# The second feed-forward stage by quarters of 256 positions instead of halves of 512, its gates and results among the steps of the delta loop

## The chip, the cores and the metric

The kernel runs on 1 core of one Trainium2 chip. The metric is the device time of the run in microseconds (us). Engines are named as in the profile: PE (matmul), DVE (vector), ACT (activations), POOL (elementwise and selects), SP (which issues most DMAs).

## The reference

Four blocks follow each other on `x` of shape (4, 1024, 256): attention, a feed-forward block, a gated delta-rule block, and the same feed-forward block again with the same weights.

```python
x = x + attn_a(layernorm(x), ...)
x = x + ffn(layernorm(x), ...)
x = x + attn_b(layernorm(x), ...)   # delta rule
x = x + ffn(layernorm(x), ...)

def ffn(x, wf, uf, bf, wi, ui, bi, wc, uc, bc, wo, uo, bo, in_c):
    c0 = broadcast(in_c)
    def step(c, xt):
        ft = sigmoid(xt @ wf.T + c @ uf.T + bf)
        it = sigmoid(xt @ wi.T + c @ ui.T + bi)
        gt = tanh(xt @ wc.T + c @ uc.T + bc)
        return ft * c + it * gt
    c_final = scan(step, c0, x)             # over the first axis
    return tanh(x @ wo.T + c_final @ uo.T + bo)
```

The recurrence of the feed-forward block runs over the first axis, the 4 batches, and is independent for each of the 1024 positions. The output of every position in every batch needs the cell after batch 3. The delta rule runs along the 1024 positions with one state per batch and head:

```python
kb = kc * bc[:, None]
A = tril(kb @ kc.T, -1)
U = solve_triangular(eye + A, vc * bc[:, None] - kb @ S, lower=True)
o = qc @ S + tril(qc @ kc.T) @ U
S = S + kc.T @ U
```

## The kernel before

Attention comes first and fills the first half of the run. The rest is `feed_and_delta`: the first feed-forward stage, the delta loop, the second feed-forward stage, with the last gates of the first stage and the first gates of the second laid among the steps of the loop. The order of all instructions on all engines is written out by hand (`tc.manual_schedule()`): each engine takes its instructions in the order in which the code issues them.

**The delta loop** (L1226) takes steps `s` from 0 to 50. A tile is 32 positions of all four batches, 32 tiles in all, and four tiles make a block of 128 positions. Step `s` makes the keys, queries, values and gates of tile `c = s` (to step 31), the score products of tile `s - 1`, and the recurrence of tile `t = s - 18` (`LAG` is 18): `from_state` (L808, 64 small matmuls with the state), `less` (L824, DVE), `solve` (L835, with the inverse loaded by `place`), `state` (L849, 32 small matmuls and a DVE sum `sb`), `within` (L862). One step behind, for tile `s - 19`, come `turn_out` (L889, two transposes of the scaled output `og`) and `result` (L907, the product with `wo`, then a POOL add; after every fourth tile `x3` is written to DRAM). The inverses of 8 tiles at a time are computed on DVE by `substitute`, cut over seven steps; the last group runs in steps 34 to 40. Steps 32 and on have no keys.

**The gates** of a feed-forward stage (`half_gates`, L929) are made for 512 positions at a time. For each batch `t` (0 to 3), each half `m` of the 256 cell features and each gate `j` (f, i, c) there is a part `begin` (L942), two matmuls 128x128 by 128x512 with the normalized input `k.xnT`, and for `t > 0` a part `end` (L956), two more with the cell of batch `t - 1` added into the same PSUM tile. The profile counts each of these matmuls twice, so a part appears as x4. `act` (L965) is the tanh on ACT, `combine` (L976) the new cell on DVE (and POOL for batch 0). Both are put off in `cells.late` and issued by `flush` at the beginning of the next part. A half has 42 parts and two that only flush. With two PSUM banks (`steps_banks`) two `begin`s stand ahead of their `end`s; with one bank they alternate.

PSUM tiles of the loop come from the pool `pps` of three buffers (tag `ps1`): the products of keys and gates, transposes, output products, norm transposes, gate tiles (in the loop) and results. `solve` has a buffer of its own (`pzu`).

**The results** of a stage: `extra` (L1030) is the product of the final cell with `uo` for 128 positions, into `e`; `residual` (L1042) loads 128 positions of all batches (512 KB); `fed` (L1047) is, for one batch, the product with `wo`, a DVE add of `e`, a tanh and a POOL add to the residual, and after batch 3 a write of 512 KB. `settle` issues the tanh and POOL adds that are owed. For positions 512 to 1023 of the second stage `ahead` (L1080) makes the products with `wo` before the cell is known, and `last_results` (L1098) adds the rest at the end.

**The second stage before the change.** The input of 128 positions `q` is loaded and normalized (`second_norm`, L1166) in two halves of two batches; `later` (L1219) gives their steps: q0 in steps 32 and 33, q1 in 34 and 35, q2 in 36 and 37, q3 in 38 and 39, q4 in 42 and 43, q5 in 46 and 47, the first half of q6 in 50. The load of q is issued three steps before its first half (L1298). `SECOND` is therefore 40: from there `half_gates(0)` gives three parts to each step through `gate_part` (L1242), in up to four slots: ahead of `solve`, behind it, behind `turn_out`, behind `result`. 33 parts are done by the end of step 50. After the loop `woven` lays the last 11 parts of the first half among the norms of q6 and q7, then `half_gates(1)` (44 parts, 42 with matmuls) among the results of q0 to q3 and the `ahead` work of q4 to q7, and `last_results` ends the run.

```python
                if s >= SECOND:
                    fill, gates = gates[:3], gates[3:]
```

Of the kernel before, what the change touches and what calls it, by code (L numbers as in the profile page):

```python
# [491 lines left out]
def feed_and_delta(k, w, out):  # L492
# [19 lines left out]
    W = TT + 1  # L512
    with ExitStack() as es:
        wp = es.enter_context(tc.tile_pool(name="d_w", bufs=1))
        hp = es.enter_context(tc.tile_pool(name="d_h", bufs=4))
        big = es.enter_context(tc.tile_pool(name="d_big", bufs=1))
        sm = es.enter_context(tc.tile_pool(name="d_sm", bufs=1))
        kp = es.enter_context(tc.tile_pool(name="d_keep", bufs=LAG))
# [407 lines left out]
        cells = Ctx()  # L926
        e = wp.tile([P, NTL // BT // 2, C], F32, name="e")

        def half_gates(n, banks, cellp):  # L929


            cells.bank, cells.late = 0, []
            of = [[] for _ in range(B)]
            cells.new = of[B - 1]

            def flush():
                now, cells.late = cells.late, []
                for a in now:
                    a()

            def begin(t, m, j):
                flush()  # L942
                if j == 0:
                    cells.act, cells.ps = [], {}
                pool, tag = banks[cells.bank % len(banks)]
                cells.bank += 1
                ps = cells.ps[j] = pool.tile([P, 512], F32, tag=tag, name="ps_gate")
                for kc in range(KC):
                    nc.tensor.matmul(  # L949
                        ps, f["w" + "fic"[j]][:, kc, ds(m * P, P)], k.xnT[:, kc, t, ds(n * 512, 512)],  # L950
                        start=kc == 0, stop=t == 0 and kc == KC - 1,
                    )
                if t == 0:
                    cells.late.append(lambda: act(t, m, j))

            def end(t, m, j):  # L956
                flush()
                for kc in range(KC):
                    nc.tensor.matmul(  # L959
                        cells.ps[j], f["u" + "fic"[j]][:, kc, ds(m * P, P)], cellp.get(of[t - 1], kc),  # L960
                        start=False, stop=kc == KC - 1,
                    )
                cells.late.append(lambda: act(t, m, j))

            def act(t, m, j):  # L965
                bias = f[("z" if t == 0 else "b") + "fic"[j]]
                a = gp.tile([P, 512], F32, tag="g", name="gate")
                nc.scalar.activation(  # L968
                    a, cells.ps[j], AF.Tanh, bias=bias[:, m : m + 1], scale=0.5 if j < 2 else 1.0
                )  # L970
                cells.act.append(a)
                if j == 2:
                    acts = cells.act
                    cells.late.append(lambda: combine(t, m, acts))

            def combine(t, m, acts):  # L976

                nc.vector.scalar_tensor_tensor(acts[1], acts[1], 1.0, acts[2], ALU.add, ALU.mult)  # L978
                new = cellp.new(of[t], m)
                if t == 0:  # L980
                    nc.vector.tensor_scalar(
                        acts[0], acts[0], 1.0, f["in_c"][:, m : m + 1], ALU.add, ALU.mult
                    )
                    nc.gpsimd.tensor_tensor(new, acts[0], acts[1], ALU.add)
                else:
                    nc.vector.scalar_tensor_tensor(
                        acts[0], acts[0], 1.0, cellp.get(of[t - 1], m), ALU.add, ALU.mult
                    )
                    nc.vector.scalar_tensor_tensor(new, acts[0], 0.5, acts[1], ALU.mult, ALU.add)

            parts = []
            for t in range(B):
                for m in range(KC):
                    first = [lambda t=t, m=m, j=j: begin(t, m, j) for j in range(3)]
                    second = [lambda t=t, m=m, j=j: end(t, m, j) for j in range(3)] if t > 0 else []
                    if len(banks) > 1 and t > 0:
                        parts += [first[0], first[1], second[0], second[1], first[2], second[2]]
                    elif t > 0:
                        parts += [a for j in range(3) for a in (first[j], second[j])]
                    else:  # L1000
                        parts += first
            parts.append(flush)
            parts.append(flush)
            return parts

        class OfRing:
# [6 lines left out]
            def get(self, cur, m):  # L1013
                return cur[m]

        class OfBlocks:


            def new(self, new, m):
                if m == 0:  # L1020
                    new.append(hp.tile([P, KC, BT, B, TT], F32, tag="h", name="cell"))
                return self.get(new, m)

            def get(self, cur, m):
                return cur[0][:, m].rearrange("p c b t -> p (c b t)")

        of_ring, of_blocks = OfRing(), OfBlocks()
        steps_banks = [(pzu, "zu"), (pps, "ps1")]

        def extra(q, cellp, new):  # L1030

            ps = pps.tile([P, C], F32, tag="ps1", name="ps_e")
            for kc in range(KC):
                nc.tensor.matmul(
                    ps, cellp.get(new, kc)[:, ds(q % 4 * P, P)], f["uo"][:, kc, :], start=kc == 0,
                    stop=kc == KC - 1,
                )
            nc.vector.tensor_tensor(e[:, q % 4, :], ps, f["bo"], ALU.add)

# [1 line left out]

        def residual(q, x, name):  # L1042

            posns[q].x = io.tile([P, B, C], F32, tag="xi", name=name)
            nc.sync.dma_start(out=posns[q].x, in_=x[:, ds(q * P, P), :].rearrange("b p d -> p b d"))

        def fed(q, b, to, bank=(pps, "ps1")):  # L1047
# [28 lines left out]
        def fed_at_once(q, b, to):  # L1076
            fed(q, b, to)()
            settle()

        def ahead(q, i):  # L1080

            p = posns[q]
# [15 lines left out]
        def last_results(new):  # L1098
# [6 lines left out]
                    out=out[ds(2 * i, 2), ds(q * P, P), :].rearrange("b p d -> p b d"), in_=x  # L1105
                )

            for q in range(NTL // BT // 2, NTL // BT):
                ps = pps.tile([P, C], F32, tag="ps1", name="ps_e")
                for kc in range(KC):  # L1110
                    nc.tensor.matmul(
                        ps, of_blocks.get(new, kc)[:, ds(q % 4 * P, P)], f["uo"][:, kc, :],
                        start=kc == 0, stop=kc == KC - 1,
                    )
                for i, (x, h) in enumerate(posns[q].ahead):
# [28 lines left out]
        def last_norms():  # L1144
# [1 line left out]
            o = Ctx()  # L1146

            def get(n):
                o.x = io.tile([P, 4, C], F32, tag="xi", name="xl")
                nc.sync.dma_start(  # L1150
                    out=o.x, in_=k.x1[B - 1, ds(n * 512, 512), :].rearrange("(n p) d -> p n d", p=P)
                )
# [20 lines left out]
        with tc.manual_schedule():  # L1173
            NQ = NTL // BT

            woven(half_gates(0, steps_banks, of_ring), last_norms())
            new = cells.new
            gates = half_gates(1, steps_banks, of_ring)
            LEAD = 12
            shadows = [lambda q=q: extra(q, of_ring, new) for q in range(NQ // 2)]  # L1180
            for q in range(2):
                shadows.append(lambda q=q: residual(q, k.x1, "x1"))
                shadows += [lambda q=q, b=b: fed_at_once(q, b, k.x2) for b in range(B)]
# [35 lines left out]
            later = {}  # L1219
            for q in range(NQ):  # L1220
                for i in range(2):
                    s = max(NTL + 2 * q + i, BT * q + LAG + 8 + i)
                    if s < NTL + LAG + 1:
                        later[s] = (q, i)
            SECOND = max(s for s, (q, i) in later.items() if q == 3) + 1
            for s in range(NTL + LAG + 1):  # L1226
                c = s if s < NTL else None
                c1 = s - 1 if 0 <= s - 1 < NTL else None
# [5 lines left out]
                normed = n < len(blocks) and i < 2  # L1234
                convolved = n < len(blocks) and i >= 2
                fill = places.get(s, [])
                if s == SECOND:
                    gates = half_gates(0, [(pps, "ps1")], of_blocks)
                if s >= SECOND:
                    fill, gates = gates[:3], gates[3:]  # L1240

                def gate_part():  # L1242
                    if fill:
# [32 lines left out]
                    keys(c)  # L1276
                else:
                    gate_part()
                substitute(s, 0.7)
                if t is not None:  # L1280
                    solve(t)
# [20 lines left out]
                    within(t)  # L1302
                    scale(t)
                if GATES <= s < GATES + 4:
                    extra(s - GATES + 4, of_ring, cells.new)
                adds = [fed(q, b, k.x2, bank) for q, b in feeding]
                if normed and i == 0:
                    stats(blocks[n], 1)
# [22 lines left out]
                if convolved:  # L1331
                    silu(n, i - 2)

            rest = [(q, i) for q in range(NQ) for i in range(2) if (q, i) not in later.values()]
            shadows = []
            for q, i in rest:
                if i == 0 and q not in [a for a, _ in later.values()]:
                    shadows.append(lambda q=q: residual(q, k.x3, "x3"))
                shadows += second_norm(q, i)
            woven(gates, shadows)  # L1340
            new = cells.new
            shadows = [lambda q=q: extra(q, of_blocks, new) for q in range(NQ // 2)]
            for q in range(NQ // 2):
                shadows.append(lambda q=q: residual(q, k.x3, "x3"))
                shadows += [lambda q=q, b=b: fed_at_once(q, b, out) for b in range(B)]
            for q in range(NQ // 2, NQ):
                shadows += [lambda q=q, i=i: ahead(q, i) for i in range(2)]
            woven(half_gates(1, steps_banks, of_blocks), shadows)
            last_results(cells.new)


# [99 lines left out]
```

## Time and profile before

| | us |
|---|---|
| median of 3 runs | 1451.28 (1450.35 to 1452.29) |
| the profiled execution | 1450.73 |
| its span, first to last instruction | 1448.9 |
| PE busy | 1360.6 |
| DVE / ACT / POOL busy | 803.8 / 681.8 / 420.8 |
| start of step 32, 40, 48 (its `from_state`) | 1140.64, 1208.62, 1287.17 |
| last gate matmul ends | 1430.16 |

All times of the profile are from one execution, and parts of it are compared with its own time. The start of a step is the first of the 64 `from_state` matmuls (L819). PE's granted clock is given as a share of full speed.

### The profile page before, as it was taken

To read this page: it belongs to the slowest core of one execution; us is meant where nothing else is said; L and a number is where in the kernel's file an instruction comes from. 1 tells how busy PE (TensorE), PEld (TensorE's weight loads), DVE (VectorE), ACT (ScalarE), POOL (GpSimd) and SP (SyncE) were. 2 spreads that over 40 slices of the span, in tenths; PEclk is the share of its full clock that TensorE was granted. 3 is DMA by queue.
4 is the path that set the end of the run, shared out by engine and by line. 5 is a ranking of instruction groups with operands and counts; after the bars stand their busy time and mean duration, and the time that the engine had idled before them with its cause. 6 is when DMAs were issued, how large, how long until landed. Compare 5 with 4: busy or idle time off the path is not lost. (4 is left out here: it accounts for less than half of the span.)

```text
span 1448.9 us, 33556 instructions
## 1 busy us (share of the span) xinstructions
PE 1360.6 (94%) x13316; PEld 660.6 (46%) x13316; DVE 803.8 (55%) x2298; ACT 681.8 (47%) x1639; POOL 420.8 (29%) x680
## 2 busy tenths in 40 slices
PE   7999999999999999999999989988788878999997
PEld 3443444434444343344344545454455555554554
DVE  5775667666676666676322333377777665233224
ACT  2365655556555656555632244455454333334222
POOL 4030002323032120021120233256676655342221
PEclk8899999999999999999999999999999769999999
DMA  3203111101110001100020121234545544221032
GB/s 95 53 16 79 17 18 43 20 2 46 32 32 17 2 17 31 32 17 2 17 74 15 44 66 52 67 95 107 132 117 121 127 117 97 55 66 44 29 92 97
DMA packets 117804, 79.78 MB, mean 55 GB/s; under 512 B 58960, under 2 KB 114768, under 8 KB 117648
## 3 DMA queue, kind: packets, MB, share of 16 engines
q1 hardware_dynamic: 115616, 76.33, 21.2%
q8 instruction: 105, 1.72, 0.5%
q10 hardware_dynamic: 2032, 1.31, 0.3%
q14 instruction: 51, 0.42, 0.1%
HBM read 41.37 MB, written 27.59 MB: 48 GB/s over the span
## 5 line engine op out<-in xcount | busy, mean ns | idle before, releaser
L337 ACT ACTIVATE p<-ps_s 128x512 f32<-128x512 f32 (+3 forms) x768 | 334.0, 491 | 249.0 <-PE ps_s L325 215.8
L325 PE MATMUL ps_s<-k,q 32*128 32x512 f32 (+3 forms) x1536 | 393.4, 541 | 2.7 <-DVE m L341 1.1
L330 PE MATMUL ps_s<-q,k 32*128 32x512 f32 (+3 forms) x1536 | 351.0, 532 | 0.0
L347 DVE TENSOR_REDUCE m<-ps_s 128x1 f32<-128x512 f32 x256 | 163.9, 685 | 83.3 <-PE ps_s L325 76.9
L341 DVE CUSTOM_DVE_ANT_0 junk<-ps_s,mask,m 128x512 bf16<-128x512 f32 (+3 forms) x256 | 128.1, 548 | 71.8 <-PE ps_s L325 70.9
L379 PE MATMUL ps_y<-p,vb 128*32 128x512 f32 (+3 forms) x1536 | 163.3, 498 | 1.2 <-ACT ys L385 1.2
L325 PEld LDWEIGHTS ps_s<-k,q 32*128 32x128 f32 x1536 | 149.4, 185 | 26.0 <-issue 9.4
L330 PEld LDWEIGHTS ps_s<-q,k 32*128 32x128 f32 x1536 | 121.7, 183 | 81.0 <-DVE m L347 20.1
L341 DVE CUSTOM_DVE_ANT_0 junk<-ps_s,mask 128x512 bf16<-128x512 f32 (+3 forms) x256 | 114.8, 487 | 72.9 <-PE ps_s L325 60.1
L403 POOL TENSOR_TENSOR xa<-xa,yt 128x256 f32<-128x256 f32 x32 | 23.3, 728 | 312.9 <-DVE yt L399 300.0
L322 PEld LDWEIGHTS <-identb 128*128 128x128 bf16 x512 | 34.6, 98 | 116.0 <-issue 112.4
L164 POOL TENSOR_SCALAR rs<-mv 128x2 f32<-128x2 f32 x24 | 5.5, 228 | 272.1 <-DVE mv L163 272.1
L379 PEld LDWEIGHTS ps_y<-p,vb 128*32 128x32 f32 x1536 | 30.6, 108 | 105.2 <-issue 92.0
L655 PE MATMUL ps_kqv<-wa,h 128*128 128x512 f32 x128 | 67.3, 642 | 8.2 <-ACT h L645 8.2
L322 PE MATMUL ps_s<-mb,identb 128*128 128x128 bf16 x512 | 71.4, 223 | 0.3 <-ACT p L337 0.3
L978 DVE SCALAR_TENSOR_TENSOR gate<-gate 128x512 f32<-128x512 f32 x32 | 22.8, 712 | 85.5 <-ACT gate L968 85.5
L1063 POOL TENSOR_TENSOR x<-x,hh 128x256 f32<-128x256 f32 x48 | 37.5, 787 | 98.4 <-ACT hh L1062 75.1
L1058 DVE TENSOR_TENSOR hh<-ps_h,e 128x256 f32<-128x256 f32 x48 | 20.2, 420 | 80.0 <-PE ps_h L1052 73.0
L949 PE MATMUL ps_gate<-xnT,ffn_wf 128*128 128x512 f32 x128 | 61.0, 599 | 1.0 <-DVE yt L399 1.0
L949 PE MATMUL ps_gate<-xnT,ffn_wc 128*128 128x512 f32 x128 | 60.8, 597 | 0.1
L949 PE MATMUL ps_gate<-xnT,ffn_wi 128*128 128x512 f32 x128 | 60.4, 594 | 0.0
L169 POOL TENSOR_SCALAR xn<-xa,mv,rs 128x256 f32<-128x256 f32 x48 | 58.4, 1225 | 2.5
(208 smaller groups left out, 2172.4 us busy)
## 6 DMA issues: line engine op xcount, KB each, us to landing
x<-x SPq DMA_DIRECT2D x28, 512.0 KB
kept<-gs SPq DMA_DIRECT2D x32, 192.0 KB
gl<-kept SPq DMA_DIRECT2D x32, 192.0 KB
x<-xa SPq DMA_DIRECT2D x8, 512.0 KB
xb<-x SPq DMA_DIRECT2D x32, 128.0 KB
xr<-x SPq DMA_DIRECT2D x32, 128.0 KB
x<-xr SPq DMA_DIRECT2D x32, 128.0 KB
k<-kall SPq DMA_DIRECT2D x60, 64.0 KB
```

Of the source, the lines that this page charges most:

```text
L169: nc.gpsimd.tensor_scalar(xn, bt.xa[:, c + i, :], mv[:, i, 0:1], rs[:, i : i + 1], ALU.subtract, ALU.mult)
L322: nc.tensor.matmul(ps[:, :P], identb, mb, start=True, stop=True)
L325: nc.tensor.matmul(ps[:, :n], first.q[rows(j), ds(qt * P, P)], first.k[rows(j), ds(c0, n)], start=True, stop=True,)
L330: nc.tensor.matmul(ps[:, :n], second.k[rows(j), ds(kt * P, P)], second.q[rows(j), ds(half * 512 + q0, n)], start=not diag, stop=True, skip ...
L337: nc.scalar.activation(p[:, j, q0:], ps[:, :n], AF.Exp)
L341: nc.vector.tensor_tensor_reduce(out=junk[:, :n], in0=ps[:, :n], in1=mask[:, 512 - n :], scale=1.0, scalar=-3e38 if qt < 4 else first.m0[: ...
L347: nc.vector.tensor_reduce(first.m0[:, j, qt - 4 : qt - 3], ps[:, :n], AX.X, ALU.max)
L379: nc.tensor.matmul(u.y[ds(32 * j, 32), q0:], vb[u.b % 2][:, kt, 4 * u.g + j, :], u.p[s][:, j, q0:], start=kt == 0, stop=last,)
L403: nc.gpsimd.tensor_tensor(xs, xs, yt.rearrange("p n j d -> p n (j d)"), ALU.add)
L655: nc.tensor.matmul(dst, hT(c, kc), wt[:, kc, :], start=kc == 0, stop=kc == KC - 1)
L949: nc.tensor.matmul(ps, f["w" + "fic"[j]][:, kc, ds(m * P, P)], k.xnT[:, kc, t, ds(n * 512, 512)], start=kc == 0, stop=t == 0 and kc == KC - 1,
L1063: nc.gpsimd.tensor_tensor(x[:, b, :], x[:, b, :], h, ALU.add)
```

## The change

- `half_gates(n)` becomes `new_gates(at, width, ...)`. The first stage calls it with 512 as before. The second calls it four times with 256 positions. The two flushes at the end move into the last part, so a list has 42 parts.
- Cells of the second stage lie in the ring `cp` (`OfPairs`, one tile of 2 x 256 for a batch) instead of in the pool of `h` (`OfBlocks`); that pool goes from 4 buffers to 3, and the residual pool (`xi`) from 2 to 3.
- `later` starts at step 28: q0 is normalized in steps 28 and 29, q1 in 30 and 31, q2 in 34 and 35, q3 in 38 and 39; the others stay.
- `second_stage(n)` makes a list of 52 parts for 256 positions: 42 gate parts, two `extra`, eight `fed_late`. The two residual loads are issued with parts 30 and 34. Such a list is begun in step 32, in 40 and in 48. Each step from 32 on takes 7 parts (even steps) or 6 (odd ones). Steps 32 and on have a second slot ahead of `solve`.
- `fed_late` issues the matmuls of one result and then the DVE add of the result before it.
- The first two lists end with steps 39 and 47. Of the third, 20 parts fall into steps 48 to 50 and 32 are laid after the loop among the norms of q6 and q7. The last 256 positions follow with two banks among the `ahead` work of q6 and q7 alone, and `last_results` deals with q6 and q7.

```diff
@@ -512,7 +512,7 @@
...
         wp = es.enter_context(tc.tile_pool(name="d_w", bufs=1))
-        hp = es.enter_context(tc.tile_pool(name="d_h", bufs=4))
+        hp = es.enter_context(tc.tile_pool(name="d_h", bufs=3))
         big = es.enter_context(tc.tile_pool(name="d_big", bufs=1))
@@ -926,7 +926,7 @@
...
-        def half_gates(n, banks, cellp):
+        def new_gates(at, width, banks, cellp):
@@ -944,10 +944,10 @@
...
                 cells.bank += 1
-                ps = cells.ps[j] = pool.tile([P, 512], F32, tag=tag, name="ps_gate")
+                ps = cells.ps[j] = pool.tile([P, width], F32, tag=tag, name="ps_gate")
                 for kc in range(KC):
                     nc.tensor.matmul(
-                        ps, f["w" + "fic"[j]][:, kc, ds(m * P, P)], k.xnT[:, kc, t, ds(n * 512, 512)],
+                        ps, f["w" + "fic"[j]][:, kc, ds(m * P, P)], k.xnT[:, kc, t, ds(at, width)],
                         start=kc == 0, stop=t == 0 and kc == KC - 1,
@@ -964,7 +964,7 @@
...
                 bias = f[("z" if t == 0 else "b") + "fic"[j]]
-                a = gp.tile([P, 512], F32, tag="g", name="gate")
+                a = gp.tile([P, width], F32, tag="g", name="gate")
                 nc.scalar.activation(
@@ -999,8 +999,8 @@
...
                         parts += first
-            parts.append(flush)
-            parts.append(flush)
+            last = parts.pop()
+            parts.append(lambda: (last(), flush(), flush()))
             return parts
@@ -1013,27 +1013,26 @@
...
-        class OfBlocks:
+        class OfPairs:
...
                 if m == 0:
-                    new.append(hp.tile([P, KC, BT, B, TT], F32, tag="h", name="cell"))
-                return self.get(new, m)
+                    new.append(cp.tile([P, KC, 256], F32, tag="cell", name="cell"))
+                return new[0][:, m]
             def get(self, cur, m):
-                return cur[0][:, m].rearrange("p c b t -> p (c b t)")
-        of_ring, of_blocks = OfRing(), OfBlocks()
+                return cur[0][:, m]
+        of_ring, of_pairs = OfRing(), OfPairs()
         steps_banks = [(pzu, "zu"), (pps, "ps1")]
-        def extra(q, cellp, new):
+        def extra(q, cellp, new, at):
...
                 nc.tensor.matmul(
-                    ps, cellp.get(new, kc)[:, ds(q % 4 * P, P)], f["uo"][:, kc, :], start=kc == 0,
-                    stop=kc == KC - 1,
+                    ps, cellp.get(new, kc)[:, ds(at, P)], f["uo"][:, kc, :], start=kc == 0, stop=kc == KC - 1
                 )
@@ -1041,7 +1040,7 @@
...
-            posns[q].x = io.tile([P, B, C], F32, tag="xi", name=name)
+            posns[q].x = io.tile([P, B, C], F32, tag="xi", name=name, bufs=3)
             nc.sync.dma_start(out=posns[q].x, in_=x[:, ds(q * P, P), :].rearrange("b p d -> p b d"))
@@ -1076,6 +1075,21 @@
...
             settle()
+        pending = [None]
+        def fed_late(q=None, b=None, to=None):
+            adds = pending[0]
+            pending[0] = fed(q, b, to) if q is not None else None
+            settle()
+            if adds is not None:
+                adds()
+        def both(*parts):
+            return lambda: [a() for a in parts]
+        LAST = (6, 7)
@@ -1105,11 +1119,11 @@
...
-            for q in range(NTL // BT // 2, NTL // BT):
+            for q in LAST:
                 ps = pps.tile([P, C], F32, tag="ps1", name="ps_e")
...
                     nc.tensor.matmul(
-                        ps, of_blocks.get(new, kc)[:, ds(q % 4 * P, P)], f["uo"][:, kc, :],
+                        ps, of_pairs.get(new, kc)[:, ds(q % 2 * P, P)], f["uo"][:, kc, :],
                         start=kc == 0, stop=kc == KC - 1,
@@ -1146,7 +1160,7 @@
...
             def get(n):
-                o.x = io.tile([P, 4, C], F32, tag="xi", name="xl")
+                o.x = io.tile([P, 4, C], F32, tag="xi", name="xl", bufs=3)
                 nc.sync.dma_start(
@@ -1173,11 +1187,11 @@
...
-            woven(half_gates(0, steps_banks, of_ring), last_norms())
+            woven(new_gates(0, 512, steps_banks, of_ring), last_norms())
             new = cells.new
-            gates = half_gates(1, steps_banks, of_ring)
+            gates = new_gates(512, 512, steps_banks, of_ring)
             LEAD = 12
-            shadows = [lambda q=q: extra(q, of_ring, new) for q in range(NQ // 2)]
+            shadows = [lambda q=q: extra(q, of_ring, new, q * P) for q in range(NQ // 2)]
             for q in range(2):
@@ -1219,10 +1233,29 @@
...
                 for i in range(2):
-                    s = max(NTL + 2 * q + i, BT * q + LAG + 8 + i)
+                    s = max(NTL - 4 + 2 * q + i, BT * q + LAG + 8 + i)
                     if s < NTL + LAG + 1:
                         later[s] = (q, i)
-            SECOND = max(s for s, (q, i) in later.items() if q == 3) + 1
+            SECOND = {NTL + 8 * n: n for n in range(3)}
+            ONCE = 7
+            def second_gates(n, banks):
+                return new_gates(256 * n, 256, banks, of_pairs)
+            def second_stage(n):
+                parts = new_gates(256 * n, 256, [(pps, "ps1")], of_pairs)
+                new = cells.new
+                pair = (2 * n, 2 * n + 1)
+                for j, q in enumerate(pair):
+                    parts[-12 + 4 * j] = both(lambda q=q: residual(q, k.x3, "x3"), parts[-12 + 4 * j])
+                parts += [lambda q=q: extra(q, of_pairs, new, q % 2 * P) for q in pair]
+                parts += [lambda q=q, b=b: fed_late(q, b, out) for q in pair for b in range(B)]
+                parts[-1] = both(parts[-1], fed_late, fed_late)
+                return parts
+            todo = []
             for s in range(NTL + LAG + 1):
@@ -1234,10 +1267,11 @@
...
                 fill = places.get(s, [])
-                if s == SECOND:
-                    gates = half_gates(0, [(pps, "ps1")], of_blocks)
-                if s >= SECOND:
-                    fill, gates = gates[:3], gates[3:]
+                if s in SECOND:
+                    todo += second_stage(SECOND[s])
+                if s >= NTL:
+                    n_ = ONCE - s % 2
+                    fill, todo = todo[:n_], todo[n_:]
@@ -1276,6 +1310,7 @@
...
                     gate_part()
+                    gate_part()
                 substitute(s, 0.7)
@@ -1302,7 +1337,7 @@
...
                 if GATES <= s < GATES + 4:
-                    extra(s - GATES + 4, of_ring, cells.new)
+                    extra(s - GATES + 4, of_ring, cells.new, (s - GATES) * P)
                 adds = [fed(q, b, k.x2, bank) for q, b in feeding]
@@ -1331,21 +1366,18 @@
...
-            rest = [(q, i) for q in range(NQ) for i in range(2) if (q, i) not in later.values()]
             shadows = []
-            for q, i in rest:
-                if i == 0 and q not in [a for a, _ in later.values()]:
-                    shadows.append(lambda q=q: residual(q, k.x3, "x3"))
-                shadows += second_norm(q, i)
-            woven(gates, shadows)
-            new = cells.new
-            shadows = [lambda q=q: extra(q, of_blocks, new) for q in range(NQ // 2)]
-            for q in range(NQ // 2):
-                shadows.append(lambda q=q: residual(q, k.x3, "x3"))
-                shadows += [lambda q=q, b=b: fed_at_once(q, b, out) for b in range(B)]
-            for q in range(NQ // 2, NQ):
+            for q in range(NQ):
+                for i in range(2):
+                    if (q, i) not in later.values():
+                        if i == 0:
+                            shadows.append(lambda q=q: residual(q, k.x3, "x3"))
+                        shadows += second_norm(q, i)
+            woven(todo, shadows)
+            shadows = []
+            for q in LAST:
                 shadows += [lambda q=q, i=i: ahead(q, i) for i in range(2)]
-            woven(half_gates(1, steps_banks, of_blocks), shadows)
+            woven(new_gates(768, 256, steps_banks, of_pairs), shadows)
             last_results(cells.new)
```

## The prediction

> **What bounds the kernel now.** I read the page first: busy times, then the forty slices.
>
> ```profile
> span 1448.9 us, 33556 instructions
> PE 1360.6 (94%) x13316; PEld 660.6 (46%) x13316; DVE 803.8 (55%) x2298; ACT 681.8 (47%) x1639; POOL 420.8 (29%) x680
> ...
> PE   7999999999999999999999989988788878999997
> ...
> PEclk8899999999999999999999999999999769999999
> ```
>
> PE is busy for 94% of the span and no other engine comes near. A change that only moves PE's work can therefore pay only where PE idles or runs slowly. The slices show one such place, from 70 to 85% of the span: PE's digit falls to 7 and 8, and in two of these slices its clock row reads 7 and 6. Next I cut the end of the run into stretches: steps 32 to 39 of the delta loop, steps 40 to 47, steps 48 to 50, what follows the loop up to the last gate matmul, and the rest. The columns are the length, the busy time of each engine, PE's granted clock and the DMA share.
>
> ```profile
> 1140.64:1208.62 67.98, 51.94 (x1394) 37.51 (x1393) 43.87 (x135) 24.88 (x59) 40.63 (x79) 0.65 0.46 111
> 1208.62:1287.17 78.55, 76.32 (x1442) 39.88 (x1441) 28.95 (x71) 26.51 (x59) 33.24 (x60) 1.00 0.33 82
> 1287.17:1313.31 26.14, 25.10 (x348) 12.99 (x348) 9.76 (x21) 8.39 (x19) 11.11 (x20) 1.00 0.07 18
> 1313.31:1430.16 116.85, 115.53 (x339) 62.81 (x338) 31.64 (x63) 30.40 (x54) 20.45 (x31) 1.00 0.21 63
> 1430.16:1448.90 18.74, 8.90 (x40) 7.11 (x39) 12.68 (x21) 5.57 (x9) 6.12 (x4) 0.87 0.33 112
> ```
>
> Steps 32 to 39 carry no gates: PE is busy 52 of 68 us at a clock of 0.65. The 117 us after the loop are solid PE work at full clock. Work taken from there and put into steps 32 to 39 shortens the run by what those steps don't grow. The timeline of PE in step 41, which already holds three gate parts, says what such a step costs (start, duration, then the instruction):
>
> ```profile
> 1217.88 0.85 PE L819 MATMUL four<-sb,kv 32*32 32x64 f32 x64
> 1218.66 1.98 PE L949 MATMUL ps_gate<-xnT,ffn_wf 128*128 128x512 f32 x4
> 1220.58 0.65 PE L842 MATMUL ps_u<-z,inv 32*32 32x64 f32 x32
> 1221.16 1.98 PE L949 MATMUL ps_gate<-xnT,ffn_wi 128*128 128x512 f32 x4
> 1223.07 0.39 PE L856 MATMUL four<-u,k 32*32 32x64 f32 x32
> 1223.40 0.44 PE L893 MATMUL ps_oT<-ident,og 128*128 128x128 f32 x2
> 1223.67 1.88 PE L949 MATMUL ps_gate<-xnT,ffn_wc 128*128 128x512 f32 x4
> 1225.48 0.65 PE L869 MATMUL four<-u,gl 32*32 32x64 f32 x32
> 1226.07 1.13 PE L911 MATMUL ps_f<-wo,oT 128*128 128x256 f32 x4
> 1227.15 0.85 PE L819 MATMUL four<-sb,kv 32*32 32x64 f32 x64
> ```
>
> From start to start the step takes 9.27 us: 3.63 of its own (0.78+0.58+0.33+0.27+0.59+1.08) and 5.64 for three gate parts, with no idle time.
>
> **The price of a part.** After the loop a 512-wide part follows the next in 1.72 us, so the three cost 5.16 and 0.48 is spent at the edges between wide and 32-row matmuls, 0.16 for each slot. With four slots, as the change uses, a step's own cost is 3.63 + 0.64 = 4.27. The 256-wide price is in the rows at the end:
>
> ```profile
> 1430.00 5.34 PE L1091 MATMUL ps_h<-ffn_wo,xnT 128*128 128x256 f32 x24
> ...
> 1233.73 1.13 PE L959 MATMUL ps_gate<-cell,ffn_uf 128*128 128x512 f32 x2 [2.17 <-POOL cell L984]
> ```
>
> 24 such matmuls take 5.2 us back to back, 0.216 each, so a part of four is 0.865, half the wide one. Halving the width is then free on PE, though it doubles the weight loads; a load takes 0.19 (rows of L949 and L959) and still fits under 0.216. If it did not fit, the added loads would cost up to 0.19 each: 84 gate parts of four loads become 168, so 336 more.
>
> A rule of the Trainium skill speaks against this: "TensorE: Matmul & The Clock Gate", Part 3, says that a weight load overlaps a matmul in flight only where their row groups differ, and all these use the whole array. By it the 336 loads would add 64 us and the kernel would come out at about 1498. The rows of L1091 contradict it, and I go by them.
>
> Smaller engines: the 256-wide tanh from PSUM and the cell update on DVE are in no row. Half of the 512-wide rows (0.687 and 0.69) is the lower bound and the whole the upper; I take 0.42, the 128x256 rows of L1062 on ACT and L829 on DVE. The POOL add of batch 0 is 0.73 (L1063). At the upper bounds a handover of a cell (one tanh, three DVE operations) takes 1.1 us more, 11 over the ten handovers that show below; at the lower 3 less in all. DVE rises in steps 32 to 39 by 24 x 0.42 + 10 x 0.42 = 14 to 58 us, less than the 87 I give those steps, so it costs nothing while PE is the longer; if that cover went, DVE's surplus would be the price.
>
> **Steps 32 to 39.** 52 parts (42 gates, 2 output-bias products, 8 results), alternately 7 and 6 a step: 10.33 and 9.46 us, eight steps 79.2. Four norm transposes stay, at 0.41 (step 43's 9.68 against 9.27): 1.6. Step 32 still has the last score products, 0.45. That is 81.2 before waits.
>
> Now the waits, since PE is in order and every wait holds up the recurrence behind it (solve, then the copy of u, state, and the DVE sum that the next step needs). First: the first gate of batch 1 stands in step 33 two parts behind the last of batch 0. Its cell passes ACT 0.6, then DVE behind that step's subtraction, then POOL 0.73 behind the output scaling; PE has one part and 0.78 to cover about 3.5: 1.8. The row above, 2.17 with a 1.26 us POOL add, is the like case. Second: from batch 1 to 2 in step 34 (part 19 two parts behind 17), ACT 0.6 and three DVE operations 1.2 against 1.3: 0.6. Third: the bias product in step 38 right behind the last gate: 0.8. Fourth: the pool of three PSUM buffers. In steps 35 and 36 a new gate opens behind the output product, and its buffer is freed by a tanh queued behind a square and a copy on ACT: 1.0 each. The rest, in norm steps and among the results, 0.8. Sum 6.0; bounds 0 and, at the seen 2.17 for four handovers plus 1.0 for a buffer in each of eight steps, 16.7. So 87.2 against 67.98: **+19.2**.
>
> **Steps 40 to 47.** The same without the 0.45: 80.8 + 6.0 = 86.8 against 78.55: **+8.3**. **Steps 48 to 50.** 20 parts: 10.33 + 9.13 (no state update) + 8.15 (step 50 has only its transposes, output product and norm) = 27.6, waits 2.0: 29.6 against 26.14, **+3.5**. **Steps 28 to 31** gain four norm transposes, 4 x 0.41: **+1.6**; their DVE statistics lie under the 1.9 us key product that follows, else 0.8 a step.
>
> **After the loop.** 32 parts remain of the third stage, 27.7, with three transposes 1.3 and waits 2.0: 31.0. The last quarter has 42 gates and 8 matmul pairs of results laid ahead: 50 x 0.865 = 43.3, waits 0.3, since two parts cover each handover there. 74.6 against 116.85: **-42.3**. The end handles two quarters' blocks, not four. Counted from the last gate: the cell at 1.9, the bias product at 2.6, four DVE additions of 0.65 by 5.2, the last tanh by 5.9, POOL's second addition of 1.6 by 7.5, and 3.6 for the output write (from the last addition's end at 1445.3 to the end of the span): 11.1 against 18.74, **-7.6**.
>
> **DMAs.** Each in-loop stage adds two 512 KB loads and two writes, in steps 36 to 39 and 44 to 47; DMA engines are 0.46 busy there. The blocks for the first two norms are loaded in steps 25 and 27. On SP the load waits for the write of the same block one step earlier; behind it stand the loads of inverses and gates for the next step, which have a step of 7.8 us to spare. A wait longer than that would reach PE through solve. The third buffer keeps results and norm blocks from blocking each other. Cost nothing, bound 2 us a stage.
>
> **Sum.** 1.6 + 19.2 + 8.3 + 3.5 - 42.3 - 7.6 = -17.3. The profiled execution took 1450.73 us, 1.8 of it outside its span, and lies 0.55 below the median: 1433.4 by it, 1434.0 by the median.
>
> **The clock** is what I trust least. In step 32 waits of at most 1.61 us were followed by a drop to 0.50, while the 2.17 us wait of step 42 left it at 1.00. Around 1075 a drop cost (1 - clock) x time = 1.7 us until it recovered. I take no drop, because the windows around the waits are full of wide matmuls; one at each first handover would add 5 us.
>
> The same page (Part 1) states that PE is slowed after an idle window of some 3.4 us. By it no wait in my sum would slow the clock; step 32 shows a drop after less, so the row stands and the 5 us stay in the range.
>
> **Rivals.** (1) *The waits are covered*, by ACT and DVE running ahead in fuller steps: all 16.3 us of waits go and the time is 1418. For it: between handovers steps 41 to 49 show no idle time. Against it: each handover there did. (2) *Slower: the PSUM buffers bound.* With six or seven parts a step among three buffers shared with five other products, every step waits in its third and fourth slot for a tanh, 2 x 1.0 in 19 steps, 38 instead of the 5 I count: 1434 + 33 = 1467. It decides from 17 us, about one wait a step more than counted. For it: one bank in the loop, and tanh issued only with the next part. Against it: from the order of the parts, most buffers are freed a slot earlier. (3) *No change*: handovers at the upper bound, 10 us more in the two stages and 5 of clock: 1449. That the gates don't land in steps 32 on is excluded by the step numbers in the code.
>
> **Chances.** Forecast (1425 to 1443) 0.53; (1) 0.20; between forecast and (3) 0.05; (3) 0.07; (2) 0.15. About 0.2%, 3 us, is what can be told from no change: faster 0.77, same 0.08, slower 0.15. The range runs from (1) to just past (3), 1418 to 1451, leaving out (2).
>
> **What would show it.** Right: steps 32 to 39 near 10 us each with the clock at 1.00; the loop's end near 1345; some 75 us of solid PE from there to the last gate; 11 us behind it. Wrong: output products or gates waiting on ACT in every step (2); the clock at 0.5 in steps 33 to 40; weight loads showing as gaps between 256-wide matmuls; solve waiting for a load of inverses.

## The result and the profile after

| | us |
|---|---|
| before, median of 4 runs | 1450.89 (1450.35 to 1452.29) |
| after, median of 4 runs | 1433.28 (1430.28 to 1435.83) |
| ratio after / before | 0.9876, 95% interval 0.9854 to 0.9899 |
| profiled execution after: time, span | 1432.08, 1430.3 |

The change makes the kernel 17.6 us faster by these medians; a second set of runs, told below, gives 14.9 (1450.27 to 1435.4). The page of the changed kernel answers to the first lines shown of before:

```profile
span 1430.3 us, 34308 instructions
PE 1347.3 (94%) x13652; PEld 708.6 (50%) x13652; DVE 804.8 (56%) x2338; ACT 692.0 (48%) x1691; POOL 422.6 (30%) x690
...
PE   7999999999999999999999979988788999999997
...
PEclk8899999999999999999999999998999999999999
```

PE has 336 matmuls more and is busy 13.3 us less: the 7 and the 6 in its clock row are gone, and the same work now runs at full clock (the run with spare work below bears this out). The weight loads grew by 48 us of busy time, which is beside the matmuls. The end of the run, cut at the same places as before (steps 32 to 39, 40 to 47, 48 to 50, the rest of the third quarter, the last quarter up to the last gate, and what follows):

```profile
1142.38:1229.58 87.20, 81.47 (x1586) 61.16 (x1585) 54.06 (x152) 31.15 (x78) 41.42 (x72) 1.00 0.42 107
1229.58:1315.07 85.49, 80.86 (x1553) 60.81 (x1552) 33.46 (x89) 31.03 (x77) 36.59 (x68) 1.00 0.35 89
1315.07:1344.89 29.82, 27.29 (x392) 21.19 (x391) 9.08 (x26) 10.69 (x26) 13.34 (x23) 1.00 0.19 54
1344.89:1376.88 31.99, 29.59 (x142) 25.24 (x141) 10.35 (x30) 12.49 (x27) 7.10 (x17) 1.00 0.20 59
1376.88:1419.20 42.32, 41.91 (x195) 35.88 (x194) 10.37 (x27) 11.99 (x26) 3.98 (x6) 1.00 0.16 50
1419.20:1430.30 11.10, 3.61 (x17) 2.84 (x15) 6.78 (x11) 2.90 (x5) 2.94 (x2) 0.79 0.27 94
```

Steps 32 to 39 grew from 68.0 to 87.2 us and run at a clock of 1.00 instead of 0.65. Steps 40 to 47 grew by 6.9 and steps 48 to 50 by 3.7. What follows the loop up to the last gate fell from 116.9 to 74.3, and the end from 18.7 to 11.1. From the start of step 32 to the end of the span it is 287.9 against 308.3: a gain of 20.3, of which 1.7 went into the later start of step 32 (1142.38 against 1140.64).

Where PE still stands still, the list of its waits from step 32 on says (total, times, longest):

```profile
PE ps_gate L959 <- DVE cell L989: 5.0, 6, 1.0
PE ps_gate L959 <- POOL cell L984: 4.2, 6, 0.8
PE ps_e L1034 <- DVE cell L989: 2.8, 3, 1.4
PE ps_h L1051 <- DVE hh L1057: 1.2, 1, 1.2
PE four L869 <- DVE sb L860: 1.1, 2, 0.6
PE ps_gate L949 <- DVE hh L1057: 0.8, 2, 0.6
PE ps_gate L949 <- ACT gate L968: 0.4, 1, 0.4
```

12.0 of these 15.5 us are waits for a cell, that of the batch before or, for the bias product `ps_e`, the last one. All fall into the three quarters whose gates use one PSUM bank; the last quarter, which has two, shows none. The waits for `z` and `u` inside the recurrence are gone, and those for `sb` fell to 1.1. In the kernel before they were:

```profile
PE four L869 <- DVE sb L860: 6.3, 7, 1.4
PE ps_u L842 <- DVE z L829: 5.4, 8, 1.6
PE four L856 <- ACT u L847: 4.3, 8, 0.5
```

The first handover, from step 32 to step 33, in PE's timeline:

```profile
1152.51 1.03 PE L949 MATMUL ps_gate<-xnT,ffn_wf 128*128 128x256 f32 x4
1153.46 0.85 PE L819 MATMUL four<-sb,kv 32*32 32x64 f32 x64
1155.09 0.70 PE L959 MATMUL ps_gate<-cell,ffn_uf 128*128 128x256 f32 x2 [0.77 <-POOL cell L984]
1156.43 0.70 PE L959 MATMUL ps_gate<-cell,ffn_uf 128*128 128x256 f32 x2 [0.65 <-POOL cell L984]
```

The first pair waits for one half of the cell, the second for the other, and everything behind them in step 33 waits too.

### The profile page after: what moved, and what is told of

Its sections match the earlier page's. It is cut to its first block, busy times and chain, and to the rows that moved or that the text cites. A ratio compares the mean times of both kernels' runs of the same rounds, so it can differ in the third digit from the quotient of the medians.

```text
span 1430.3 us, 34308 instructions
## 1 busy us (share of the span) xinstructions
PE 1347.3 (94%) x13652; PEld 708.6 (50%) x13652; DVE 804.8 (56%) x2338; ACT 692.0 (48%) x1691; POOL 422.6 (30%) x690
## 3 DMA queue, kind: packets, MB, share of 16 engines
q8 instruction: 107, 1.75, 0.5%
## 5 line engine op out<-in xcount | busy, mean ns | idle before, releaser
L978 DVE SCALAR_TENSOR_TENSOR gate<-gate 128x256 f32<-128x256 f32 (+1 forms) x48 | 26.8, 559 | 118.7 <-ACT gate L968 112.2
L1062 POOL TENSOR_TENSOR x<-x,hh 128x256 f32<-128x256 f32 x56 | 41.3, 752 | 80.2 <-ACT hh L1061 72.6
L959 PE MATMUL ps_gate<-cell,ffn_uf 128*128 128x256 f32 (+1 forms) x144 | 51.5, 469 | 14.2 <-POOL cell L984 9.2
L949 PE MATMUL ps_gate<-xnT,ffn_wi 128*128 128x256 f32 (+1 forms) x192 | 63.5, 453 | 0.8 <-DVE hh L1057 0.8
L949 PE MATMUL ps_gate<-xnT,ffn_wf 128*128 128x256 f32 (+1 forms) x192 | 63.3, 452 | 1.0 <-DVE yt L399 1.0
L949 PE MATMUL ps_gate<-xnT,ffn_wc 128*128 128x256 f32 (+1 forms) x192 | 63.8, 454 | 0.4 <-ACT gate L968 0.4
L1051 PE MATMUL ps_h<-ffn_wo,xnT 128*128 128x256 f32 x224 | 57.7, 396 | 3.2 <-DVE hh L1057 2.2
```

Source lines behind the costliest of these rows:

```text
L949: nc.tensor.matmul(ps, f["w" + "fic"[j]][:, kc, ds(m * P, P)], k.xnT[:, kc, t, ds(at, width)], start=kc == 0, stop=t == 0 and kc == KC - 1,)
L959: nc.tensor.matmul(cells.ps[j], f["u" + "fic"[j]][:, kc, ds(m * P, P)], cellp.get(of[t - 1], kc), start=False, stop=kc == KC - 1,)
L1051: nc.tensor.matmul(ps, k.xnT[:, kc, b, ds(q * P, P)], f["wo"][:, kc, :], start=kc == 0, stop=kc == KC - 1)
L1062: nc.gpsimd.tensor_tensor(x[:, b, :], x[:, b, :], h, ALU.add)
```

## The experiments

The theory: PE's work is the same wherever it stands; the gain is that work from behind the loop now fills steps in which PE idled and was slowed; waits for cells take part of it back; the shorter end adds the rest. Run times of one kernel spread by up to 12 us here, and the start of step 32 moved between 1139.3 and 1146.5 us from run to run, so beside the medians I read the stretch from there to the end.

**Steps 32 to 39 left empty.**

```diff
-            SECOND = {NTL + 8 * n: n for n in range(3)}
+            SECOND = {NTL + 8 + 8 * n: n for n in range(2)}
...
-                if s >= NTL:
+                if s >= NTL + 8:
...
             woven(todo, shadows)
+            woven(second_stage(2), [])
```

> The changed kernel, but its quarters begin in step 40: steps 32 to 39 stay empty, and the third quarter's whole list stands after the loop. Theory (the gain is work laid into steps in which PE idled at a slow clock): steps 32 to 39 fall from 87.2 us to about 66 at a clock near 0.65, and 52 parts of 0.865 us, 45 us, and some 3 us of waits come after the loop: about +26 us on the changed kernel's 1433, 1459. Rival (the gain is the shorter end, two blocks instead of four behind the last gate): the end stays at 11.1 us, so most of the gain stays: at most 1443.

Measured: 1460.57 (1455.57 to 1465.16), ratio to before 1.0073 (1.0045 to 1.0101). Steps 32 to 39 of this kernel:

```profile
1142.94:1208.46 65.52, 46.02 (x1377) 32.59 (x1376) 42.38 (x121) 18.98 (x47) 35.70 (x65) 0.71 0.47 110
```

As the theory said, to 2 us. The rival falls: the end is as short here (11.2 us), and the gain is gone. The run shows more: without the filled steps, quarters are slower than the halves of before, 1460.57 against 1451.59 beside it. The new form costs time, and only its earlier start pays for it.

**Twice the weight loads in the first stage.**

```diff
                 for kc in range(KC):
-                    nc.tensor.matmul(ps, ..., k.xnT[:, kc, t, ds(at, width)], ...)
+                    for c0 in range(0, width, 256):
+                        nc.tensor.matmul(ps[:, ds(c0, 256)], ..., k.xnT[:, kc, t, ds(at + c0, 256)], ...)
```

and the same in `end`.

> The changed kernel, with every gate matmul of the first stage (512 columns) issued as two of 256, so that 336 more weight loads are made there. Theory (a load of 0.19 us lies under a 256-wide matmul of 0.216): no change, 1433, within 3 us. Rival (the Trainium skill's rule that a load overlaps only matmuls of another row group): 336 x 0.19 = 64 us more, 1497.

Measured: 1435.78 (1430.28 to 1442.1), ratio to before 0.9906 (0.9876 to 0.9936): no change that can be told from the changed kernel's, and far from 1497. PE's timeline of the first stage in this kernel:

```profile
741.05 1.89 PE L963 MATMUL ps_gate<-cell,ffn_uf 128*128 128x256 f32 x8
742.78 1.89 PE L963 MATMUL ps_gate<-cell,ffn_ui 128*128 128x256 f32 x8
```

Eight matmuls of 256 columns in 1.73 us, where four of 512 take 1.72, as in the kernel before:

```profile
1313.31 1.88 PE L959 MATMUL ps_gate<-cell,ffn_ui 128*128 128x512 f32 x4
1315.03 1.88 PE L949 MATMUL ps_gate<-xnT,ffn_wc 128*128 128x512 f32 x4
```

The weight loads of the whole run grew by 61.6 us of busy time (708.6 to 770.2) while PE's busy time did not grow (1347.3 and 1345.9). Halving the width costs PE nothing. The rule of the Trainium skill that weight loads overlap only matmuls of another row group ("TensorE: Matmul & The Clock Gate", Part 3) does not hold for these loads: of the 64 us that it would add, none shows.

**Spare work in the empty steps of the kernel before.**

```diff
+            def spare():
+                ps = pps.tile([P, C], F32, tag="ps1", name="ps_spare")
+                for kc in range(KC):
+                    nc.tensor.matmul(ps, f["wf"][:, kc, 0:P], f["wo"][:, kc, :], ...)
...
+                if NTL <= s < SECOND:
+                    fill = [spare] * 3
```

> The kernel before, with three unused 256-wide products (0.865 us each, 20.8 us in all) added to each of steps 32 to 39. Theory (these steps are long because PE idles and so runs at half clock; with work in the gaps the clock stays at 1.00 and the step is 3.63 + 0.48 + 2.6 + 0.4 for the norm = 7.2 us, step 32 about 10): 68.0 us become about 61, so 1444 in spite of the added work. Rival (the steps are bound by the chain through DVE and ACT at any clock, and added PE work delays it): between no change and +20 us, 1451 to 1471.

Measured: 1448.54 (1444.17 to 1450.3), ratio 0.9979 (0.9960 to 0.9998). Steps 32 to 39:

```profile
1141.38:1205.72 64.34, 58.48 (x1490) 42.36 (x1489) 46.01 (x135) 25.16 (x59) 41.66 (x79) 1.00 0.48 118
```

With 20.8 us of work added these steps became 3.6 us shorter, at a clock of 1.00. Without the added 20.8 us PE is busy for 37.7 us with the work that took 51.94 at a clock of 0.65. The sign is the theory's; the size is half of it. At full clock the waits for DVE remain (1.75 us for `sb` in step 34, some 0.2 to 0.4 in later ones), so the rival has a share: part of these steps' length is the chain through DVE. For the change both matter little, since 6 or 7 parts a step cover that chain.

**No waits for cells.**

```diff
-                        cells.ps[j], f["u" + "fic"[j]][:, kc, ds(m * P, P)], cellp.get(of[t - 1], kc),
+                        cells.ps[j], f["u" + "fic"[j]][:, kc, ds(m * P, P)],
+                        cellp.get(of[t - 1], kc) if width == 512 else f["wo"][:, kc, :],
```

and a slice of `wo` for the cell in the bias products of the second stage.

> The changed kernel, whose second stage takes a constant table in place of the cells in the second matmuls of its gates and in the bias products (this leaves the recurrence over batches out of the second stage, while all cells are still computed). Theory (PE's waits for cells are paid in full): the waits for cells of the trace go, 3.8 us in each of the first two stages and 4.4 in the third, 12 us in all: 1421. Rival (other chains need that time anyway, and waits move elsewhere): 1430 to 1433.

Measured: 1419.99 (1414.52 to 1421.4), ratio 0.9792 (0.9749 to 0.9835); from step 32 to the end 273.7 us against 287.9. The waits are paid in full, and 2 us more than their sum went with them. The list of waits counts idle time alone; the same 3875 matmuls from step 32 on also count 3.5 us less of busy time here (261.25 against 264.74), which suggests that a wait costs somewhat more than its idle time.

**Four blocks behind the last gate.**

```diff
-        LAST = (6, 7)
+        LAST = (4, 5, 6, 7)
...
+                if n == 2:
+                    return parts
                 new = cells.new
                 pair = (2 * n, 2 * n + 1)
```

> The changed kernel, with the results of the third quarter moved to the end: their products with wo are laid ahead among the last gates, and their bias, tanh, additions and writes follow the last gate as in the kernel before (they take the bias of the last quarter's cells, so positions 512 to 767 of the output are not the reference's). Theory (the 7.6 us at the end come from two blocks instead of four): the stretch behind the last gate grows from 11.1 to 18.7 us and PE's work stays the same, so about 1441. Rival (the end is bound by the last write, however many blocks stand before it): no change, 1433.

Measured: 1430.6 (1426.88 to 1438.66), ratio 0.9862 (0.9839 to 0.9885): far from the 1441 of the theory and near the rival's 1433, but without the changed kernel beside it. So both were run side by side:

> The changed kernel itself, beside the next two on one chip. Theory: from the start of step 32 to the end 288 us again, and a ratio to the kernel before of 0.988.

> The kernel with four blocks at the end once more, beside the changed kernel on one chip. Its trace showed 15.1 us behind the last gate instead of 11.1, and a wait of 1.4 us for the first bias product gone. Theory (the end costs 4.0 us more, of which 1 to 2 are given back by the waits): 2 to 3 us slower than the changed kernel. Rival (the end costs nothing in time): equal.

Measured: the changed kernel 1435.4 (1431.92 to 1435.94), ratio 0.9887 (0.9872 to 0.9902), and 289.4 us from step 32 to the end; with four blocks at the end 1431.25 (1426.53 to 1435.48), ratio 0.9866 (0.9845 to 0.9888). The intervals overlap. The changed kernel came out as expected, to 1.4 us in the stretch. For the other, the times do not bear out the 2 to 3 us of the theory; equal times, the rival, are not ruled out. The last window of the second kernel:

```profile
1417.83:1432.90 15.07, 5.34 (x25) 4.30 (x23) 10.28 (x17) 5.35 (x9) 6.12 (x4) 0.79 0.41 140
```

Two more blocks lengthen the stretch behind the last gate by 4.0 us, not by 7.6. The other 3.6 of the change's gain at the end go with what stands between the last gate and the bias product. PE's rows there, in the kernel before (two) and in the changed kernel (two):

```profile
1435.17 0.60 PE L1111 MATMUL ps_e<-ffn_uo,cell 128*128 128x256 f32 x2
1436.06 3.29 PE L1111 MATMUL ps_e<-ffn_uo,cell 128*128 128x256 f32 x14 [0.28 <-DVE cell L989]
...
1419.20 1.89 PE L1105 MATMUL ps_h<-ffn_wo,xnT 128*128 128x256 f32 x8
1420.92 1.89 PE L1125 MATMUL ps_e<-ffn_uo,cell 128*128 128x256 f32 x8
```

Before, 24 matmuls with `wo` came first (from 1430.00, the row of L1091 in the prediction), and the last cell update stood behind four of their additions in DVE's queue: the bias product began 5.2 us after the start of those matmuls, and its second half, which needed the cell, 6.1 us after it. With the new end eight matmuls come first and the bias product begins after 1.7 us, in this kernel with four blocks too. PE's matmuls and the place of the cell update changed together, and no run has one without the other. The whole stretch from step 32 took 290.3 us in this kernel, 0.9 more than in the changed kernel beside it and 2.4 more than in that kernel's first profile: the 4.0 are partly returned where the third quarter's bias products no longer wait (the waits of `ps_e` fell from 2.8 to 1.4 us). The 4 us by which its median is the lower do not show in this stretch of the profiled execution, and where they come from remains open.

**Results between the next quarter's gates.** If waits for cells cost 12 us, independent work put into the handovers should win them back. This version holds the results of a quarter back and lays them among the gates of the next:

```diff
+                def of(q, b):
+                    cells.flush()
+                    adds = fed(q, b, out)
+                    settle()
+                    adds()
...
+                gates = new_gates(256 * n, 256, [(pps, "ps1")] if n < 3 else steps_banks, of_pairs)
...
+                loads, biases, res = owed_results(n - 1, was)
...
+                parts = gates[:3] + biases + gates[3:6] + res[:3] + gates[6:18] + res[3:6] + gates[18:30]
+                if n < 3:
+                    return parts + res[6:] + gates[30:]
...
-                    n_ = ONCE - s % 2
+                    n_ = ONCE - s % 2 if s >= NTL + 8 else 5 + (s % 4 == 0)
```

`flush` ahead of each result issues the tanh and the cell update that are put off, so that they run while PE makes the result.

> A version that lays each quarter's bias products and results among the gates of the next quarter, where a batch's cell is handed on (two after the first three gates, then three, three and two results after the last gate of each batch), instead of behind its own gates; steps 32 to 39 then hold the 42 gate parts alone, five or six a step. Theory (PE's waits for cells, 12 us, are paid in full, and PE's work is the same wherever it stands): most of the 12 us go and a few come back in the emptier steps 32 to 39: about 1425. Rival (the fuller steps 32 to 39 matter more, as there is idle time again with 5 parts): 1433 to 1440.

> The version with the results laid between the next quarter's gates once more, beside the changed kernel on one chip. Theory: 13 us faster than the changed kernel, as the stretches from step 32 to the end (274.9 and 287.9 us) say. Rival (the difference of the medians, 14 us, came from the chips): within 4 us.

Measured: 1418.94 (1418.72 to 1420.93), ratio 0.9793 (0.9776 to 0.9810), and again 1418.5 (1417.07 to 1420.84), ratio 0.9776 (0.9762 to 0.9790), the second beside the changed kernel's 1435.4: 17 us faster, more than the 13 of the stretches in the expectation. The stretches of these two profiles themselves differ by 15.5 (289.4 and 273.9). The waits from step 32 on, in its first profile:

```profile
PE ps_gate L961 <- DVE cell L991: 2.7, 2, 1.7
PE ps_gate L951 <- issue: 1.0, 1, 1.0
PE ps_gate L961 <- POOL cell L986: 1.0, 2, 0.8
PE four L869 <- DVE sb L860: 0.5, 2, 0.4
PE ps_u L842 <- DVE z L829: 0.2, 1, 0.2
```

Only the first quarter, which has no results to lay between, still waits for cells: 3.7 us. In steps 40 to 47, and from step 48 to the bias products at the end, PE is solid:

```profile
1222.13:1301.75 79.62, 79.46 (x1553) 61.24 (x1552) 32.35 (x91) 30.84 (x77) 37.99 (x69) 1.00 0.42 108
1301.75:1409.40 107.65, 107.51 (x772) 92.20 (x772) 37.42 (x96) 38.92 (x88) 27.93 (x49) 1.00 0.19 57
```

Of the kernels that compute the whole reference this is the fastest, 2.1 to 2.2% below the one before.

## Why the prediction was right

The forecast was 1434.0 and the time is 1433.28; the sum was -17.3 and the medians differ by 17.6. That the two are so close is partly luck: the terms as measured add up to -18.6, the second set of runs gave -14.9, and single runs of the changed kernel spread by 5.6 us. Term by term, from the two profiles:

| term | predicted | measured |
|---|---|---|
| steps 28 to 31 (measured: start of step 32) | +1.6 | +1.7 |
| steps 32 to 39 | +19.2 | +19.2 |
| steps 40 to 47 | +8.3 | +6.9 |
| steps 48 to 50 | +3.5 | +3.7 |
| after the loop, to the last gate | -42.3 | -42.5 |
| behind the last gate | -7.6 | -7.6 |

The first row is safer from the steps themselves, since the start of step 32 moves from run to run: steps 28 to 31 took 34.53 us instead of 32.62, 1.9 more. In steps 40 to 47 the listed waits came to 4.6 us where 6.0 were charged.

**The step price held, to 2%.** Step 35 without its transposes and step 37 take 9.27 us (from 1176.34 to 1186.05 less 0.44, and from 1197.31 to 1206.58), for which 9.46 was predicted; 0.865 for a part was right, and so was the choice of the row over the rule on weight loads. The price charged 0.16 for an edge at each of four slots, but the parts behind `result` follow its wide matmuls: 3.63 + 3 x 0.16 + 6 x 0.865 is 9.30.

**The waits held as a sum, not one by one.** In steps 32 to 39 the first handover took 1.42 (predicted 1.8), the second 0.82 (0.6), the bias product 0.69 (0.8). The third, from batch 2 to 3, took 0.86 where I had none, a result waited 1.19 for its buffer, and step 32 waited 0.56 for `sb`. The step that failed is the pool of three PSUM buffers: I charged 1.0 us in steps 35 and 36, and neither shows a wait. In step 35 the gate opens at 1183.79 while the tanh that I had it wait for runs on ACT only from 1184.26:

```profile
1181.54 0.37 ACT L895 COPY oT<-ps_oT 128x256 f32<-128x256 f32 x1 [0.98 <-PE ps_oT L893]
...
1183.79 1.03 PE L949 MATMUL ps_gate<-xnT,ffn_wf 128*128 128x256 f32 x4
...
1183.99 0.37 ACT L913 COPY f<-ps_f 128x256 f32<-128x256 f32 x1 [0.60 <-PE ps_f L911]
1184.26 0.48 ACT L968 ACTIVATE gate<-ps_gate,ffn_bc 128x256 f32<-128x256 f32 x1
```

So it must have taken another buffer, and the one of the transposes was free since 1181.9. I had taken the buffers strictly in turn. In the sum this error, and the edge that was charged too much, were made up for by the third handover, the results and `sb`.

**The small engines.** The 256-wide tanh from PSUM takes 0.47, a cell update on DVE 0.42, where I took 0.42 for both. DVE is busy 54.1 us of the 87.2, predicted 58, and is far from full.

**The end** came out at 11.1 as worked out, with the cell at 1.9 as in the sum. The reason that the prediction names, two quarters' blocks instead of four, is half of it: 4.0 of the 7.6 us belong to the number of blocks, and 3.6 go with the earlier bias product (fewer matmuls ahead of it on PE, and the cell update ahead of the additions on DVE).

**The clock** stayed at 1.00 through all waits of steps 32 to 50, the longest 1.2 us.

**The rivals.** That the waits are covered (1418) was wrong for this change and is what the version with results in between reaches. That the PSUM buffers bind (1467) fell: no output product waits in any step, and the listed waits for a buffer (those for `hh` and for `gate`) are 2.4 us, not 38. No change (1449) would have needed longer handovers and a slowed clock.

## What to carry to other kernels

Moving work pays by what the place it goes to doesn't grow: price the new place by a step of the loop that already holds such work, not by idle percentages. Cutting a stage finer is worth it for the earlier start, and each handover between the pieces that nothing covers is then paid in full on an engine that takes its instructions in the order of the code, until independent work (here the results of the piece before) stands between producer and consumer, with the producer's late steps issued ahead of it. A slowed clock hides room: eight loop steps took in 20.8 us of matmuls and became shorter.

## What the runs showed of the hardware

256-wide fp32 matmuls with a new 128x128 weight load each follow one another at 0.216 us, as fast by the column as 512-wide ones; the load of 0.19 lies wholly beside them. PE's clock fell to 0.5 in step 32 of the kernel before after waits of at most 1.61 us among small matmuls, while 2.17 us of waiting among wide ones (step 42) left it at full speed. The rows show it; the third number from the end is the clock:

```profile
1142.00:1143.00 1.00, 0.00 (x0) 0.00 (x0) 0.93 (x5) 0.27 (x1) 0.92 (x2) 1.00 0.77 54
1143.00:1144.00 1.00, 0.40 (x19) 0.40 (x22) 1.00 (x5) 0.00 (x0) 1.00 (x3) 0.85 0.73 181
1144.00:1145.00 1.00, 0.64 (x25) 0.40 (x16) 0.86 (x5) 0.31 (x1) 0.85 (x2) 0.50 1.06 208
...
1232.00:1234.00 2.00, 0.27 (x1) 0.27 (x2) 0.00 (x0) 0.00 (x0) 1.58 (x3) 1.00 0.00 0
1234.00:1236.00 2.00, 2.00 (x38) 0.91 (x38) 0.42 (x1) 0.36 (x2) 0.00 (x0) 1.00 0.00 0
```

With 2.6 us of spare wide work in each of steps 32 to 39 it stayed at 1.00 there. Times of one kernel spread by up to 12 us (1430.28 to 1442.1 in one), and part of it arises ahead of the changed part: in the profiles of the kernels derived from the changed one, step 32 starts between 1139.3 and 1146.5 us. Why was not tried.
